# A gated cross-attention and mixture-of-experts layer on one core: the end of the kernel in the arms of its switch, router work at another point of the layers, other rows and queues for some transfers

## The chip, the cores and the metric

The kernel runs on one core of a Trainium2 chip. The metric is the device time of one execution in microseconds (us), median of several runs. A profile of one execution is used to read where the time goes; its times count from the first instruction of the span.

The core has five engines that run side by side and wait for one another through semaphores: TensorE (PE; its weight loads are shown as PEld), VectorE (DVE), ScalarE (ACT), GpSimd (POOL) and SyncE (SP). SP does no arithmetic; it issues most of the transfers. Each engine takes its instructions in order: one that waits holds all that stand behind it on its engine.

## The reference, cut to what matters

```python
# x: (16, 256, 512), ctx: (16, 256, 512); E = 8 experts, K = 2
q = layernorm(x) @ Wq;  k, v = split(ctx @ Wkv)
x = x + tanh(g_xattn) * softmax(q k^T / sqrt(512)) v
n = layernorm(x)
probs = softmax(n @ gate_w + gate_b, axis=1)        # over the tokens of a batch entry
vals, idx = top_k(probs, 2)
h = relu(n @ w1[e] + b1[e]);  h = relu(h @ w2[e] + b2[e]);  y = relu(h @ w3[e] + b3[e])
v[e] = sum over all tokens that chose e of their weight * y[e]   # one vector per expert
out = for each token the sum of v over its two experts
x = x + tanh(g_ffn) * out
```

There are 4096 tokens, so 8192 (token, expert) pairs. The kernel works out an expert only for the tokens that chose it. The sum over the tokens gives one vector of 512 numbers for each expert, and the output adds two of these vectors to every token's row. In the reference the sums are taken over the whole input (`'ebso,bse->eo'`), so nothing can be written out before the last expert is done.

## The kernel before, in words

**Attention, groups of 512 tokens.** `NG` = 8 groups (two batch entries each) are worked one after another. For a group `now` the kernel computes scores for both entries (`scores(now, 0)`, `scores(now, 1)`, L748), stores the exponentials to memory and loads them back in another layout (`send_exps`, `bring_exps`; L796, L802), forms the values (`all_values`), mixes (`mix`, matmuls L824, addition to the row L829), normalises the new rows and stores them as `tokens` (`normalise`, L205, L210), and reads them back in quarters (`xq`, L215). The group before it, `last`, goes through the router in between: `turn_rows` (a transposing DVE instruction, L226), `logits` (L236), `soften`, `divide`, `show_probs`, `choose` (13 small DVE instructions, L272 to L294), `count`, `place` (L311 to L318 and eight indirect stores on POOL, L321, which enter the tokens into `lists`).

**Experts, blocks of 528 entries.** The lists are cut into blocks of `SB` = 528 entries of one expert each. `tabulate` (L349 to L396, small DVE instructions) works out which expert and which place of the lists each block has. It is done three times, as lists fill: `tabulate_early` after group 6's attention for blocks 0 to 2 (from the copy `lists_a`), `tabulate_more` for blocks 3 and 4 (from `lists_m`), `tabulate_rest` for the rest. There are at least `NF` = 16 blocks; any beyond that (up to 7) are in a switch at the end (`tc.Switch`, L1175) whose arm 0, for none, is empty of work. In this input the arm taken is arm 0.

A block's way in: `load_tokens` (SP reads an entry of `table` into a register and loads `who`, L446), `gather` (POOL, five indirect loads L468 into `xr`), `send_rows` (store to `block`, L478 and L482), `bring_rows` (four loads `xr_q`, L487), `turn` (DVE, L226).

**A layer.** Every block runs three layers of the function `layer`. Each multiplies 512 x 512 weights with 512 x 528 rows by seven products of quarters (each eight matmuls of 128 x 264, L1019), with sums and differences on DVE ahead (`sub` for the four t, `sums` for the weights of the next layer) and additions and copies behind. The order within a layer is written out by hand (`manual_schedule` for PE, ACT, DVE and SP). The part that matters here, as PE, DVE and ACT see it:

```python
ps_y = pair("w")
for o in range(2):
    add(ps_y[o], ps_z[o], u2[:, o, :])          # DVE, L527
product(ps_x, s3, t3, False)                    # PE
for o in range(2):
    nc.scalar.copy(u3[:, o, :], ps_x[o])        # ACT, L1050
    add(out(1, 1, o), ps_z[o], u3[:, o, :])     # DVE, L527
    put(1, 1, o, out(1, 1, o))                  # ACT, L1030
product(ps_y, s4, half(1, 1), False)            # PE
# two put(0, 1, o): ACT; then `late`; then product(ps_x, part(w,1,1), t4) and two put(1, 0, o): ACT reads ps_x
```

The two banks of `ps_x` are used again by the first product of the next layer. The layer takes lists of foreign work for DVE: `first` and `second` (between the subs), `early` (after the subs), `late` (after the additions).

**Before block 0**: after the loop over groups, the last group's attention and the router of group 6 are interleaved by hand; `mix` calls `turn(held[0], rows[0], 0)` after its second tile; four matmuls at L1127 read `held[0]` ahead of block 0's first product.

**The end.** After the switch: a product and a reduction (L1218, L1223) sum the blocks of each expert, L1231 adds two parts, four transposes (L1237) and a scaling (L1241) give `v_sb`; for each of 8 groups four matmuls (L1250) form the additions, DVE adds three of the four tiles to the rows (L1259), ACT copies the fourth (L1256) and POOL adds it (L1257); one 1 MB store for each group (L1261), SP and ACT taking turns.

**The beginning.** SP issues the loads of `wq` and `wk` in turns (L588, L589); ACT's queue begins with the small loads of the gates and the router's weights (L141 to L154) and the Tanh (L144).

## Time and profile before

| | |
|---|---|
| median of three runs | 1005.53 us (1005.03 to 1010.96) |
| the profiled execution's own time | 1010.59 us |
| its span, first to last instruction | 1008.9 us |
| PE busy | 965.2 us |
| DVE busy | 695.3 us |
| ACT busy | 370.2 us |
| POOL busy | 182.6 us |
| data moved | 176.45 MB |
| mean granted TensorE clock | 0.986 |

The profiled execution is one of the longer ones: its time is near the highest of the three runs. A share of busy time is an average over stages: attention up to about 360 us, the 16 blocks from there to 972 us, the end from there. In a row of the timeline the first number is the start, the second the duration; what stands in brackets is the idle time of that engine just before, and what ended it. In the list of waits the numbers are the total in us, how often, and the longest.

### The profile page before, as it was taken

The numbers are of one execution on the slowest core, as the hardware profiler recorded it, in microseconds if no ns is written. First come the engines' busy times: TensorE is split into PE (matmuls) and PEld (weight loads), VectorE is DVE, ScalarE is ACT, GpSimd is POOL, SyncE is SP. The second block draws the span as 40 slices with busy tenths as digits, with TensorE's granted clock in tenths as the row PEclk, the third lists the DMA queues.
The fourth block names the chain that finished last, engine by engine and source line by source line (L and its number), as shares of the span: only waits on it lengthen the run. The fifth ranks groups of instructions, "written<-read, shape, count | busy, mean of one in ns | idle before, by whom it ended". The sixth has DMA issues, their size and how long they took to land. (4 is left out here: it accounts for less than half of the span.)

```text
span 1008.9 us, 12597 instructions
## 1 busy us (share of the span) xinstructions
PE 965.2 (96%) x4208; PEld 769.3 (76%) x4208; DVE 695.3 (69%) x1487; ACT 370.2 (37%) x874; POOL 182.6 (18%) x212
## 2 busy tenths in 40 slices
PE   7999999999999889999999999999999999999964
PEld 3677878778787367788788888888888888888851
DVE  3467677686777587776886676766776676676735
ACT  1222223122232124344444444444444444444421
POOL 2000330312303441205022102202202201100003
PEclk9999999999999999999999999999999999999987
DMA  7256536465475798759668667667757757756109
GB/s 265 71 166 179 135 117 186 137 179 143 137 189 129 209 237 233 202 164 177 170 201 207 164 198 199 172 195 194 182 185 194 186 181 194 199 168 150 64 5 333
DMA packets 156159, 176.45 MB, mean 175 GB/s; under 512 B 38929, under 2 KB 94225, under 8 KB 156050
## 3 DMA queue, kind: packets, MB, share of 16 engines
q1 hardware_dynamic: 145442, 153.42, 55.4%
q0 software_dynamic: 7680, 17.90, 6.9%
q10 hardware_dynamic: 2960, 4.21, 1.2%
q8 instruction: 36, 0.59, 0.2%
q14 instruction: 41, 0.34, 0.1%
HBM read 136.33 MB, written 39.77 MB: 175 GB/s over the span
## 5 line engine op out<-in xcount | busy, mean ns | idle before, releaser
L1019 PE MATMUL ps_x<-t,s 128*128 128x264 f32 x768 | 186.7, 386 | 1.6 <-ACT ps_w L1037 1.6
L1019 PEld LDWEIGHTS ps_x<-t,s 128*128 128x128 f32 x768 | 145.8, 190 | 26.9 <-ACT ps_w L1037 2.0
L468 POOL DMA_INDIRECT xr<-tokens,at_b x80 | 83.5, 1044 | 196.6 <-DMA block<-xr 174.1
L1030 ACT ACTIVATE h<-ps_w,bias 128x264 f32<-128x264 f32 x192 | 86.2, 474 | 44.2 <-PE ps_w L1019 44.2
L1019 PE MATMUL ps_z<-t,w_e 128*128 128x264 f32 x384 | 93.4, 386 | 0.5 <-DVE t L530 0.5
L527 DVE TENSOR_TENSOR ps_w<-ps_z,u 128x264 f32<-128x264 f32 x96 | 41.8, 440 | 75.5 <-ACT h L1030 75.4
L1019 PE MATMUL ps_x<-t,w_e 128*128 128x264 f32 x384 | 93.3, 386 | 0.0
L321 POOL DMA_INDIRECT lists<-pairs,idx x64 | 62.9, 983 | 162.6 <-DVE hot L314 122.4
L1041 ACT COPY u<-ps_x 128x264 f32<-128x264 f32 x96 | 36.4, 379 | 132.2 <-PE ps_x L1019 132.2
L1019 PEld LDWEIGHTS ps_z<-t,w_e 128*128 128x128 f32 x384 | 72.8, 190 | 13.4 <-DVE t L530 0.9
L1019 PEld LDWEIGHTS ps_x<-t,w_e 128*128 128x128 f32 x384 | 73.0, 190 | 12.5
L527 DVE TENSOR_TENSOR h<-ps_z,u 128x264 f32<-128x264 f32 x96 | 41.5, 432 | 56.1 <-ACT u L1050 56.1
L530 DVE TENSOR_TENSOR s<-w_e 128x512 f32<-128x512 f32 x96 | 66.1, 689 | 11.5 <-DMA w_e<-in_L_ffn_w 9.9
L1030 ACT ACTIVATE h<-h,bias 128x264 f32<-128x264 f32 x96 | 49.4, 515 | 52.6 <-DVE h L527 52.6
L1019 PE MATMUL ps_w<-h,s 128*128 128x264 f32 x256 | 62.4, 387 | 3.3 <-DVE ps_w L527 3.3
L1019 PE MATMUL ps_x<-h,w_e 128*128 128x264 f32 x256 | 62.3, 386 | 0.0
L1019 PE MATMUL ps_w<-h,w_e 128*128 128x264 f32 x256 | 62.2, 386 | 0.0
L530 DVE TENSOR_TENSOR t<-h 128x528 f32<-128x528 f32 x64 | 45.2, 706 | 20.5 <-ACT h L1030 19.8
L1019 PEld LDWEIGHTS ps_w<-h,s 128*128 128x128 f32 x256 | 48.5, 190 | 12.3 <-DVE ps_w L527 4.1
L1037 ACT COPY ps_w<-ps_x 128x264 f32<-128x264 f32 x96 | 34.8, 363 | 61.7 <-PE ps_x L1019 60.7
L748 PE MATMUL sc<-wide,wide 128*128 128x256 f32 x256 | 56.6, 379 | 0.0
L824 PE MATMUL mm<-v,eT 128*128 128x512 f32 x128 | 56.2, 592 | 0.0
(178 smaller groups left out, 1554.4 us busy)
## 6 DMA issues: line engine op xcount, KB each, us to landing
w_e<-in_L_ffn_w SPq DMA_DIRECT2D x48, 1024.0 KB, 7.3
xr_q<-block SPq DMA_DIRECT2D x64, 272.0 KB, 9.0
block<-xr SPq DMA_DIRECT2D x16, 1024.0 KB, 8.6
early<-in_x_t SPq DMA_DIRECT2D x8, 1024.0 KB, 8.1
wide<-in_ctx_t SPq DMA_DIRECT2D x8, 1024.0 KB, 6.2
x<-in_x SPq DMA_DIRECT2D x8, 1024.0 KB, 5.9
tokens<-xn SPq DMA_DIRECT2D x32, 256.0 KB, 3.6
xq<-tokens SPq DMA_DIRECT2D x32, 256.0 KB, 5.1
```

Source lines behind the costliest of these rows:

```text
L321: ins = nc.gpsimd.indirect_dma_start(out=lists, out_offset=at, in_=pairs[:, s.g * TG + t, i, :], in_offset=None)
L468: tc.keep_in_program_order(nc.gpsimd.indirect_dma_start(out=r.rows[:n, t, :], out_offset=None, in_=src, in_offset=bass.IndirectOffsetOnAxi ...
L527: nc.vector.tensor_tensor(out, a, b, ALU.add)
L530: nc.vector.tensor_tensor(out, a, b, ALU.subtract)
L748: nc.tensor.matmul(sc[:, t, :], qT[:, c, q0 : q0 + P], s.ctxT[:, c, b * S : (b + 1) * S], start=(c == 0), stop=(c == NC - 1),)
L824: nc.tensor.matmul(ps, s.eT[b][:, k, own * P : (own + 1) * P], s.v[:, b * ST + k, :], start=(k == 0), stop=(k == ST - 1),)
L1019: nc.tensor.matmul(ps[o], a[:, k, o * P : (o + 1) * P], b[:, k, :], start=(first and k == 0), stop=(k == 1), skip_group_check=True,)
L1030: nc.scalar.activation(out(a, j, o), ps, AF.Relu, bias=x.bias[:, c : c + 1])
L1037: nc.scalar.copy(ps_w[o], ps_x[o])
L1041: nc.scalar.copy(u2[:, o, :], ps_x[o])
```

## The change

In words:

- **The end in the arms.** What stood after the switch (`summed`, the transposes, the scaling, the writing out) is now a function `write_out(n)`, called in each of the eight arms. A hint of the switch's target is issued on all five engines ahead of block 15 (`tc.switch_hint`). The sum over blocks 0 to 14 (`sum_most`) stands between layers 1 and 2 of block 15. In arm 0 the last block's share is one product of 128 x 32 without a reduction. The scaling is cut in two halves, DVE and ACT.
- **The order of the last transfers.** Group 0 is stored tile by tile, group 1 in halves, the others whole, by ACT and SP in turns, the even groups' store being issued by ACT after its copy for the next group; the tile that POOL adds comes first in groups 1 to 7.
- **4 KB rows.** A partition now holds two neighbouring rows of `x`, so that loads of `x` and stores of the output move 4 KB at a time (the 256 KB stores of group 0 keep 2 KB). The host permutes `x_t` to match.
- **Queues at the beginning.** `wk` is loaded by ACT's queue, the gates' and the router's small loads come after it.
- **A new place for router work in a layer**: `mid`, after the two additions into `ps_y` and before those into `out(1, 1, o)`. The second use of `tabulate` is cut in two, block 0 and block 1, layer 1 (before: ahead of block 0); `turn_rows` of the last group goes from `early` to `mid` in block 0, layer 2; `soften` from `early` to `second` in block 1, layer 0, `divide` from `late` to `mid` there; `choose` from block 1, layer 1, `early`, to layer 2, `mid`; `place` in block 2, layer 1, from `early` to `mid`; the two parts of `tabulate_rest` in block 3, layers 0 and 1, from `late` to `mid`. The `who` and the gather for block 3 are issued after layer 1 of block 1.
- **The way into block 0.** `lists_a` is copied inside `normalise`, between the stores of `tokens` and the loads of `xq`; `turn_rows(last)` stands between the two scores of the last group; the exponentials' store and load stand ahead of the first weights; `who` and the first gather ahead of them.

The core of the diff:

```diff
     def load_x(g):
-        nc.sync.dma_start(xg[g], x_f[...].rearrange("(t p) d -> p t d", p=P))
+        nc.sync.dma_start(xg[g].rearrange("p (b k) d -> p b k d", k=ST), as_held(x_f, g))
...
-                nc.sync.dma_start(wk_sb[:, c, :], weight(wk_t)[:, c, :])
+                nc.scalar.dma_start(wk_sb[:, c, :], weight(wk_t)[:, c, :])
...
         projections()
+        load_gates()
...
-            normalise(now)
+            normalise(now, [copy_lists] if g == GA else [])
...
+        scores(now, 0)
+        turn_rows(last)
         for b in range(NA):
             who[b] = load_tokens(b)
         rows[0] = gather(0, who[0])
+        send_exps(now, 0)
+        bring_exps(now, 0)
+        scores(now, 1)
+        send_exps(now, 1)
+        bring_exps(now, 1)
         weights[0] = open_expert(0)
         load_layer(weights[0])
-        for b in range(BG):
-            scores(now, b)
-            send_exps(now, b)
-        bring_exps(now, 0)
         send_rows(rows[0])
-        bring_exps(now, 1)
         rows[1] = gather(1, who[1])
-        turn_rows(last)
         logits(last)
...
-        tabulate_more()
...
             for o in range(2):
                 add(ps_y[o], ps_z[o], u2[:, o, :])
+            for work in mid:
+                work()
             product(ps_x, s3, t3, False)
...
+        tables = tabulate_more()
         block = one(0, NF, {
...
-            "early2": [lambda: turn_rows(now)],
+            "mid1": [lambda: next(tables)], "mid2": [lambda: turn_rows(now)],
         })
...
         block = one(1, NF, {
-            "early0": [lambda: soften(now)], "late0": [lambda: divide(now)],
-            "early1": [lambda: choose(now)],
+            "second0": [lambda: soften(now)], "mid0": [lambda: divide(now)],
+            "mid1": [lambda: run(tables)], "mid2": [lambda: choose(now)],
         })
         next(block)
         show_probs(now)
+        next(block)
+        who[NA] = load_tokens(NA)
+        rows[NA] = gather(NA, who[NA])
         run(block)
-        block = one(2, NF, {"early1": [lambda: place(now)]})
+        block = one(2, NF, {"mid1": [lambda: place(now)]})
...
-        block = one(3, NF, {"late0": [lambda: next(tables)], "late1": [lambda: run(tables)]})
+        block = one(3, NF, {"mid0": [lambda: next(tables)], "mid1": [lambda: run(tables)]})
...
-            for b in range(NM, NF):
+            for b in range(NM, NF - 1):
                 run(one(b, NF))
+            tc.switch_hint({e: extras for e in (PE, DVE, ACT, POOL, SP)}, NB - NF + 1, label="rest")
+            block = one(NF - 1, NF)
+            next(block)
+            next(block)
+            vT, most = sum_most()
+            run(block)
             flush(NC)
-        for n in tc.Switch(extras, NB - NF + 1):
+        for n in tc.Switch(extras, NB - NF + 1, hint="rest"):
...
+            was = list(used)
+            write_out(n)
+            used[:] = was
```

The new functions of the end, cut:

```python
def write_out(n):
    if n:
        rest = summed(vpart[:, :, NF - 1 : NF + n], own[:, NF - 1 : NF + n, :])
    else:
        rest = top(1, NC, E)
        nc.vector.tensor_tensor(rest, <column NF-1 of vpart>, <row NF-1 of own>, ALU.mult)
    nc.vector.tensor_tensor(vT[:, :, :, :E], most, rest, ALU.add)     # broadcast
    ...                                                              # 4 transposes into halves
    nc.vector.tensor_scalar(v_sb[:, :n], halves[0][:, :n], gate[:, 1:2], None, ALU.mult)
    nc.scalar.activation(v_sb[:, n:], halves[1][:, :n], AF.Identity, scale=gate[:, 1:2])

    def store(g, t):
        b, k = divmod(t, ST)
        rows, out = xg[g].rearrange("p (b k) d -> p b k d", k=ST), as_held(o_f, g)
        if g == 0:
            nc.sync.dma_start(out[:, b, k], rows[:, b, k])
        elif g == 1:
            if k == ST - 1:
                nc.sync.dma_start(out[:, b], rows[:, b])
        elif t == TG - 1:
            (nc.sync if g % 2 else nc.scalar).dma_start(out, rows)
```

## The prediction

> **What bounds the kernel now.** I read the page's busy times first, then the list of waits for TensorE's own idle time, then the timeline around each of these waits, then the chain and the stretches of the end.
>
> ```profile
> PE 965.2 (96%) x4208; PEld 769.3 (76%) x4208; DVE 695.3 (69%) x1487; ACT 370.2 (37%) x874; POOL 182.6 (18%) x212
> ```
>
> PE is the bound: an edit gains only where PE stands idle, and costs wherever it makes PE wait. The waits of PE (engine, waited for: us in total, times, longest):
>
> ```profile
> PE mm L607 <- DMA wide<-in_wk_t: 7.1, 1, 7.1
> ...
> PE vps L1237 <- DVE room L1231: 7.0, 1, 7.0
> ...
> PE ps_w L1127 <- DVE x L829: 4.9, 1, 4.9
> ...
> PE pt L236 <- DVE xnT L226: 3.3, 1, 3.3
> ...
> PE ps_w L1019 <- DVE ps_w L527: 3.3, 2, 2.1
> ...
> PE ps_x L1019 <- ACT ps_w L1037: 1.6, 1, 1.6
> ...
> PE out_ps L1250 <- DVE room L1241: 0.9, 1, 0.9
> ...
> PE ps_z L1019 <- DVE t L530: 0.5, 1, 0.5
> ```
>
> They sum to 28.6 us, and the end without PE (993.9 to 1008.9) is the rest. Only 5.4 us (3.3 + 1.6 + 0.5) lie inside the expert blocks. The 7.0 at L1237 is explained by the chain:
>
> ```profile
> 972.30 0.07 DVEq L1308
> 972.37 3.82 issue
> 976.19 0.63 DVE room L1218
> ```
>
> DVE is done at 972.0, branches, and stands for 3.82 us with nothing to wait for. After that the store bounds (us, busy times with counts, PEclk, DMA share, GB/s):
>
> ```profile
> 984.00:986.00 2.00, 2.00 (x14) 1.16 (x12) 2.00 (x4) 0.26 (x1) 1.27 (x1) 0.75 0.55 207
> 986.00:988.00 2.00, 2.00 (x15) 0.92 (x9) 2.00 (x5) 1.17 (x2) 1.22 (x1) 1.00 1.03 373
> ...
> 1000.00:1002.00 2.00, 0.00 (x0) 0.00 (x0) 0.00 (x0) 0.00 (x0) 0.00 (x0) 0.50 1.04 368
> ```
>
> From 985 to 1007.3 the transfers are full at some 376 GB/s, so the end is: when the first byte leaves, plus 8.39 MB at that rate.
>
> **The beginning: -1.0 us.** PE starts at 7.05, when the first quarter of wk is there; its load is issued at 1.26, behind that of wq at 0.81. On ACT's queue, with the small gate loads behind it, it is issued at about 0.81: -0.45. DVE's own three operations on wq run from 4.64 to 6.04, so PE could start there, some 1.0 sooner, if wk's quarter lands with wq's. Bounds: 0 (same engines, nothing lands sooner) and -1.6 (wq sooner too). I take -1.0. The Tanh, now later, is hidden: its reader, L777, is first needed at 47.8. A rule speaks against more than the first figure: the Trainium skill, page "DMA: Bandwidth & Descriptors", section "Issuing engines are not separate DMA queues", says that transfers issued from several engines share the same 16 DMA engines and that only issue time is saved. By it the term would be -0.45 and the total below -5.9 instead of -6.4.
>
> **The way into block 0: -3.8 us.** Here lie the waits of 3.3 and 4.9.
> - The router's matmuls wait until 331.67 for `turn_rows`, which runs 329.30 to 331.61 behind the second maximum. Moved ahead of it, it can start when `xq` is there: four loads issued 320.29 to 322.20, 5.1 to landing, so 327.3; plus 2.31 is 329.6, against 328.4 when the scores end. 2.1 of 3.3 goes.
> - Ahead of the additions of L829 DVE runs `tabulate_more` from 349.10 to 354.34. Without it, additions follow PE's tiles. What is late next is `xr_q`: `turn(held[0])` needs it before the last two additions. `lists_a` is copied before the `xq` loads and not behind them, so `who` can be issued at 325.9, when the table is written (before: 328.91), and the gather some 3 us sooner. But SP now passes two round trips of exponentials (2.3 + 2.1 each) and 1 MB of weights before the store of `block`: I get that store at about 339.5 (before 342.30), its landing behind the weights, `xr_q` issued at 346.6 (before 347.31) and landed 8 later at 354.5. Turn 1.31, two additions 1.37: L1127 starts at about 357.0 instead of 360.25. That is -3.3, the 2.1 within it.
> - After the 4.9 us wait PE runs slow: the four matmuls at L1127 take 647 ns each (2.1 us), the first eight of L1019 2.76 against 1.94. After the 3.3 us wait it did not: L236's sixteen took 1.92 as always. With a wait near 3.5 left, I take a quarter of the 1.9 us: -0.5.
>
> Bounds: 0 (rows no sooner) and -7.5 (both waits nearly gone, clock kept).
>
> **The new place `mid`: +6.2 us net, the term that decides.** What follows it in a layer (timeline of block 15, layer 1):
>
> ```profile
> 953.50 0.44 DVE L527 TENSOR_TENSOR ps_w<-ps_z,u 128x264 f32<-128x264 f32 x1 [0.45 <-ACT h L1030]
> ...
> 954.29 0.43 DVE L527 TENSOR_TENSOR h<-ps_z,u 128x264 f32<-128x264 f32 x1 [0.35 <-ACT u L1050]
> ...
> 954.75 0.51 ACT L1030 ACTIVATE h<-h,bias 128x264 f32<-128x264 f32 x1 [0.50 <-DVE h L527]
> 955.17 0.36 ACT L1050 COPY u<-ps_x 128x264 f32<-128x264 f32 x1
> 955.57 0.43 DVE L527 TENSOR_TENSOR h<-ps_z,u 128x264 f32<-128x264 f32 x1 [0.85 <-ACT u L1050]
> ...
> 957.43 0.48 ACT L1030 ACTIVATE h<-ps_x,bias 128x264 f32<-128x264 f32 x1
> ...
> 958.12 1.94 PE L1019 MATMUL ps_x<-h,w_e 128*128 128x264 f32 x8
> ```
>
> At `mid` DVE idles 0.35. Work there delays the first addition into h, and ACT works in order: behind that addition stand its Relu, the second copy, the second addition, three more Relus, and last the Relu that frees `ps_x` (957.43, ends 957.91). PE's next layer starts into `ps_x` at 958.12. Where the addition is late already (480.36 in block 2) that Relu follows it by 2.89 us, against 3.15 here: 0.26 of slack. With 0.14 between the Relu's end and PE (0.2 less a hand-over) and the 0.45 by which a DVE that doesn't wait is sooner (0.34 from addition to addition, against 0.79), 0.85 us at `mid` is free, and the rest moves PE one for one.
>
> Durations, start to start, from this trace: first part of `tabulate_more` 2.86 (349.10 to 351.96), second 2.38, `choose` 2.80 (424.03 to 426.83), `place` 2.60 (from 461.56), the parts of `tabulate_rest` 2.62 (495.40 to 498.02) and 3.13 (507.36 to 510.49). Sum 16.4, less 6 x 0.85: +11.3. Free: `divide` (0.5), and `turn_rows` in block 0, layer 2 (2.3), since PE has the router's 1.92 us next, which don't use `ps_x`.
>
> Against it go the waits that the old places made: 2.08 (block 0, `turn_rows` in `early`), 1.63 (block 1, `soften`), 0.49 (block 3), and most of 1.23 in block 2, where weights landed 3.8 late and will not if PE comes later: -5.1 with 0.9 of the last. At their old places `choose`, `place` and the second part of `tabulate_rest` cost PE nothing. Bounds of the term: -5.4 (`mid` costs nothing) and +8.
>
> In block 1 SP reads the table for block 3 only when `mid` of layer 1 has written it, at about 430 on the old clock; behind it stand the weights of layer 2, which went out at 432.2 before: hidden, with 2 us to spare.
>
> **The end: -7.8 us.**
> - The stall of 3.82 goes: after the first branch the engines were in arm 0 within 0.5 us; the one that stalls is the second, out of the arm, and the work now comes before it. At its new place it lies behind the last store's issue, under some 8 us of transfers. -3.8. If that cover fails it is back.
> - The last block's sum 0.62 + 0.42 becomes one of some 0.19 (128 x 32, as L294): -0.85; the scaling 0.75 becomes two halves of 0.45 side by side: -0.3. `sum_most` (1.03 + 0.65 before) goes where DVE idles 1.32 before the t of layer 2, 2 us ahead of need: nothing.
> - Group 0's first store leaves after one DVE addition (982.53) and not after POOL's (983.98): -1.4. Adding 256 KB takes 0.6, moving it 0.7, so the transfers stay full.
> - PE's clock was 0.50 there after 7 us of idling; with 2.5 us it may stay: 0 to -0.8, I take -0.4.
> - 4 KB rows for 7.34 of 8.39 MB. No row shows such a store. The nearest, 4.2 KB pieces of `wbc`, are slower (0.54 MB in 26.2% of 6.5 us: 319 GB/s); copies of 18.8 KB reached 442 in their best slice (`lists_a`). Bounds +3.5 and -2.9; near the first lies a single transfer's start and end, so I take -1.0.
>
> Sum -7.75. Bounds -2.5 and -11.
>
> **Sum.** -1.0 - 3.8 + 6.2 - 7.8 = -6.4 us. From the profiled execution's 1010.59 (span 1008.9 and 1.69 around it) that gives 1004.2; this execution is 5 above the median of the runs, whose 1005.53 gives 999.1.
>
> **Rivals.**
> 1. *`mid` is free.* The values added there, out(1, 1), are needed only by the second product of the next layer, and DVE is idle 31% of the time. Against: the Relus in one line on ACT. The term is -5.1 instead of +6.2: 987.8.
> 2. *The rows of block 3 come too late (slower).* Their gather was issued at 413 to 419, 26 us ahead of their store at 445.2; now `who` is read at 430.4, the gather ends at 439.6 and lands 8.4 later, at 448, when the store is due, with PE 3.5 later. If POOL holds it as long as its longest wait for `block` (17.3 us), it lands near 465; SP waits with weights and `xr_q` behind it, which have 6 us to spare: some 11 us, and 1010. The total is slower than before from 455 on.
> 3. *The branch still costs.* The exit, or a fetch in block 15 displaced by the hint, takes 3.8 again: 1002.9.
>
> **Numbers.** The forecast 0.50 (its own range 993 to 1003), rival 1 0.25, rival 2 0.12, rival 3 0.13. Low end 987 from rival 1, high end 1007 between rivals 3 and 2. One per cent, about what a measurement tells, is 10 us: faster by more holds for nearly all of rival 1 and the forecast's low end, 0.33; slower by more for a part of rival 2, 0.07; within it 0.60.
>
> **What would show it.** PE waits of 1.5 to 2.3 us for an ACT Relu at the start of the layer after each of the six `mid` works (`ps_x` L1019 <- ACT h), 11 us in all; no 3.82 issue in the chain; first store some 10 us after the last product (before 13.2); the end at more than 376 GB/s; L1127's wait near 3.5. No such PE waits, or a wait of SP for the gather into `xr` in block 2, would make the forecast wrong.

## The result, and the profile after

The changed kernel takes 1014.89 us (median of 6 runs, 1012.79 to 1018.80) against 1007.65 of the kernel before (median of 6, 1005.03 to 1010.96). The ratio is 1.0076, with a 95% interval of 1.0047 to 1.0105: slower, where the forecast was 6.4 us faster. The profiled execution took 1013.73 us (span 1011.9). The six runs of the changed kernel spread with PE's mean granted clock (three at 0.987 to 0.988 took 1012.8 to 1013.7, three at 0.983 to 0.984 took 1016.1 to 1018.8), while the 87 runs of the kernel before that stand beside the experiments show no such relation.

The busy time of PE, from the first part of the page of the changed kernel:

```profile
PE 965.3 (95%) x4208; PEld 767.1 (76%) x4208; DVE 693.9 (69%) x1485; ACT 369.2 (36%) x875; POOL 185.5 (18%) x212
```

PE is busy for as long as before (965.2). So the loss is to be looked for in its idle time, and the list of waits of PE in the changed kernel (engine, waited for: us in total, times, longest) says where:

```profile
PE ps_w L1235 <- DVE x L834: 14.5, 1, 14.5
PE mm L612 <- DVE early L608: 6.1, 1, 6.1
PE ps_x L1028 <- ACT h L1039: 5.8, 6, 1.0
PE ps_x L1028 <- ACT u L1061: 2.7, 5, 1.1
PE ps_x L1188 <- DVE room L1180: 2.3, 1, 2.3
PE pt L242 <- DVE xnT L232: 0.7, 1, 0.7
PE out_ps L1216 <- ACT room L1193: 0.6, 1, 0.6
```

Line numbers have moved: L612 was L607, L242 was L236, L1235 was L1127, L1028 was L1019, L1188 was L1237. Three of the four parts went the way that was forecast: PE starts 0.95 sooner, the wait for the sum at the end is 2.3 and not 7.0, and the new stalls of `mid` are there, 8.5 us in this list. The fourth, the way into block 0, went the other way: the router's wait is 0.7 and not 3.3, but the wait ahead of block 0, forecast at 3.5, is 14.5. The queue of SP shows why. The rows of block 0 go through it twice: they are stored to `block`, and when that store has landed they are loaded again as `xr_q`. Its timeline in the changed kernel (start, time to issue):

```profile
339.74 0.40 SPq L523 DMA_DIRECT2D w_e<-in_L_ffn_w  x1
340.32 0.38 SPq L483 DMA_DIRECT2D block<-xr  x1
340.75 0.49 SPq L487 DMA_DIRECT2D block<-xr  x1
354.04 1.93 SPq L492 DMA_DIRECT2D xr_q<-block  x4
356.21 1.36 SPq L523 DMA_DIRECT2D w_e<-in_L_ffn_w  x2
```

the same store and load in the kernel before:

```profile
342.30 0.38 SPq L478 DMA_DIRECT2D block<-xr  x1
342.77 0.45 SPq L482 DMA_DIRECT2D block<-xr  x1
...
347.31 1.91 SPq L487 DMA_DIRECT2D xr_q<-block  x4
```

and two pieces of the chain that ended last in the changed kernel (start, us, what):

```profile
340.75 13.21 DMA block<-xr
355.48 7.82 DMA xr_q<-block
```

The store of `block` is issued two microseconds earlier than before (340.75 and not 342.77) and lands 6.7 later: 13.2 us, where the old order needed 4.5. `xr_q` can only be issued then, and DVE, which has nothing else to do, waits 13.6 us for it.

The end, in stretches (us; busy time with counts of PE, PEld, DVE, ACT, POOL; PEclk, DMA share, GB/s):

```profile
984.00:986.00 2.00, 1.38 (x12) 0.74 (x15) 0.48 (x1) 0.47 (x1) 0.00 (x0) 1.00 0.04 8
...
988.00:990.00 2.00, 2.00 (x14) 0.90 (x10) 2.00 (x5) 0.59 (x1) 2.00 (x3) 1.00 1.03 381
...
1000.00:1002.00 2.00, 0.00 (x0) 0.00 (x0) 0.69 (x2) 0.12 (x1) 1.26 (x1) 0.64 1.05 397
```

PE's clock stays at 1.00 behind the wait (before, in the stretch where the transfers began, 0.75), and the full stretches move 381 to 414 GB/s, where those of before moved 368 to 397. From the last product to the end of the span it is 30.3 us, 38.1 before.

### The profile page after: what moved, and what is told of

Read it like the earlier page. It is cut to its first block, busy times and chain, and to the rows that moved or that the text cites. A ratio compares the mean times of both kernels' runs of the same rounds, so it can differ in the third digit from the quotient of the medians.

```text
span 1011.9 us, 12632 instructions
## 1 busy us (share of the span) xinstructions
PE 965.3 (95%) x4208; PEld 767.1 (76%) x4208; DVE 693.9 (69%) x1485; ACT 369.2 (36%) x875; POOL 185.5 (18%) x212
## 4 chain that ended last, share of the span: by engine, by line
PE 85%; DVE 5%; DMA 3%; ACT 2%; POOL 2%; issue 1%; SPq 1%; DVEq 0%; ACTq 0%; POOLq 0%
PE ps_x L1028 32%; PE ps_w L1028 16%; PE mm L665 14%; PE ps_z L1028 8%; PE sc L753 5%; PE mm L829 4%; ACT h L1039 2%; PE mm L612 2%; PE mm L740 1%; DMA block<-xr 1%; PE pt L242 1%; PE out_ps L1216 1%; POOL lists L327 1%; DMA xr_q<-block 1%; DMA exps<-ex 1%
## 5 line engine op out<-in xcount | busy, mean ns | idle before, releaser
L1028 PE MATMUL ps_x<-t,s 128*128 128x264 f32 x768 | 186.6, 386 | 0.0
L1028 PEld LDWEIGHTS ps_x<-t,s 128*128 128x128 f32 x768 | 145.9, 190 | 25.0
L473 POOL DMA_INDIRECT xr<-tokens,at_b x80 | 86.3, 1079 | 195.7 <-DMA block<-xr 173.1
L1028 PE MATMUL ps_x<-t,w_e 128*128 128x264 f32 x384 | 94.9, 388 | 2.7 <-ACT u L1061 2.7
L1028 PE MATMUL ps_z<-t,w_e 128*128 128x264 f32 x384 | 93.3, 386 | 0.0
L1028 PEld LDWEIGHTS ps_x<-t,w_e 128*128 128x128 f32 x384 | 72.4, 190 | 17.4 <-ACT u L1061 5.4
L1028 PEld LDWEIGHTS ps_z<-t,w_e 128*128 128x128 f32 x384 | 73.0, 190 | 12.5
L1028 PE MATMUL ps_x<-h,w_e 128*128 128x264 f32 x256 | 62.8, 388 | 4.8 <-ACT h L1039 4.8
L1028 PE MATMUL ps_w<-h,w_e 128*128 128x264 f32 x256 | 62.2, 386 | 0.0
L1028 PE MATMUL ps_w<-h,s 128*128 128x264 f32 x256 | 62.2, 386 | 0.0
L1028 PEld LDWEIGHTS ps_x<-h,w_e 128*128 128x128 f32 x256 | 46.6, 189 | 16.4 <-ACT h L1039 6.9
```

The source lines that it names most:

```text
L473: tc.keep_in_program_order(nc.gpsimd.indirect_dma_start(out=r.rows[:n, t, :], out_offset=None, in_=src, in_offset=bass.IndirectOffsetOnAxi ...
L1028: nc.tensor.matmul(ps[o], a[:, k, o * P : (o + 1) * P], b[:, k, :], start=(first and k == 0), stop=(k == 1), skip_group_check=True,)
```

## Experiments

All ratios are to the kernel before, run on the same chip; "changed kernel" is the one above. Waits are those of each run's own trace, in us, by the line numbers of the changed kernel.

| run | ratio (95%) | wait L242 | wait L1235 | waits for ACT in L1028 |
|---|---|---|---|---|
| changed, again | 1.0069 (1.0049 to 1.0088) | 1.0 | 13.8 | 8.5 |
| block first | 1.0021 (1.0006 to 1.0037) | 1.0 | 9.7 | 8.5 |
| scatter later | 1.0051 (1.0027 to 1.0074) | 1.1 | 10.2 | 8.6 |
| rows first | 1.0003 (0.9986 to 1.0020) | 1.3 | 3.2 (+1.9 for weights) | 8.6 |
| rows first, scatter later | 1.0009 (0.9994 to 1.0024) | 0.9 | 2.9 (+0.9) | 8.8 |
| whole old order | 0.9958 (0.9945 to 0.9971) | 3.3 | 1.0 | 8.6 |
| old queue, early `turn_rows` | 0.9979 (0.9963 to 0.9995) | 1.0 | 3.4 | 8.5 |
| old places | 1.0002 (0.9984 to 1.0020) | 1.2 | 14.1 | 1.4 |
| `mid` behind | 0.9969 (0.9955 to 0.9983) | 0.8 | 14.1 | 0 |
| 2 KB rows | 1.0091 (1.0057 to 1.0125) | 1.4 | 14.0 | 8.6 |
| no hint | 1.0081 (1.0056 to 1.0105) | 1.0 | 14.4 | 8.5 |
| rows first + places | 0.9902 (0.9868 to 0.9937) | 1.1 | 3.5 (+1.1) | 0 |
| ... + weights ahead | 0.9881 (0.9855 to 0.9907) | 1.0 | 3.9 | 0 |
| old queue + places | 0.9887 (0.9871 to 0.9904) | 0.9 | 3.4 | 0.2 |
| whole old order + places | 0.9873 (0.9854 to 0.9893) | 3.3 | 1.0 | 0.3 |

### The kernel before, a second profile

> The kernel before, once more, for a second profile of it. The profiled execution of before took 1010.59 us where its other runs had a median of 1005.5, so the traces of before and after differ by 3 us where the runs differ by 7. If that execution was a slow one, this profile's time is 1005 to 1007, and its waits of PE show which of those read before were larger than usual (3.3 at L236, 4.9 at L1127, 2.1 and 1.6 at L1019). If profiled executions are slower in general, it is again about 1010. Ratio 1.000.

The profiled execution took 1011.01, ratio 0.9995 (0.9982 to 1.0008). Neither guess holds cleanly: the profiled execution is the highest of its ten, but profiled executions of other kernels (1007.14 of 1005.81 to 1012.36, 996.73 of 996.73 to 999.24) are not high. The runs of before in all these comparisons lie between 1004.3 and 1011.7; what makes the whole of that spread stays open. What the second profile does show is which waits were those of one execution. Its waits of PE:

```profile
PE pt L236 <- DVE xnT L226: 3.9, 2, 3.3
PE ps_w L1127 <- DVE x L829: 3.8, 1, 3.8
PE ps_w L1019 <- DVE ps_w L527: 1.5, 2, 0.8
PE ps_x L1019 <- ACT ps_w L1037: 1.4, 1, 1.4
```

The 2.1 us that the forecast put down to `turn_rows` in `early` of block 0 is gone, though `turn_rows` stands at the same place. In the first profile DVE's waits between 385 and 402 show what was different, a late transfer that `turn_rows` reads; the second has no such wait:

```profile
DVE xnT L226 <- DMA xq<-tokens: 2.5, 1, 2.5
```

### The way into block 0

Block first. The edit:

```
-        weights[0] = open_expert(0)
-        load_layer(weights[0])
         send_rows(rows[0])
+        weights[0] = open_expert(0)
+        load_layer(weights[0])
```

> The changed kernel with one thing different: `block`'s store (send_rows) stands ahead of the first MB of weights on SP's queue, and not behind it. Theory 1 (the new hand order puts the store behind the weights; in the changed kernel it was issued at 340.75 and landed at 353.98, PE then waited 14.5 us at L1235): the store lands within 5 us of its issue, at about 345, `xr_q` at about 353, the wait at L1235 falls from 14.5 to 2 to 5 us, and the ratio to the kernel before from 1.0076 to about 0.997. Theory 2 (the scatter of `place`, which now runs at the same time as the store, slows it): the store still lands at 350 or later, the wait stays above 9 us, and the ratio above 1.003.

Scatter later. The edit moves `place(last)` from behind `count(last)` to behind `figures_left = mix(...)`:

> The changed kernel with one thing different: `place` of group 6 comes only after the additions in front of L1235, so that its scatter no longer runs beside `block`'s store; the weights stay ahead of the store. It puts 2.6 us of DVE in front of block 0's first sums. Theory 1 (behind the weights): the store still lands at about 352, the wait at L1235 stays at 12 to 15 us, some 2 us are lost behind it, and the ratio is 1.007 to 1.011. Theory 2 (the scatter): the store lands at about 346, the wait falls under 7 us, and the ratio is about 1.001.

Neither theory got its numbers. The chain of the first of these two kernels, then of the second:

```profile
339.50 7.03 DMA block<-xr
...
348.06 10.98 DMA xr_q<-block
```
```profile
341.30 8.08 DMA block<-xr
...
350.91 8.69 DMA xr_q<-block
```

The 13.2 us of the store (11.5 in the second profile of the changed kernel) fall to 7.0 in the one and to 8.1 in the other. So taking away the weights ahead of it or the scatter beside it wins some 5 to 6 us, and what is left still keeps it at 7 to 8, where a store with neither takes 4.5. (In the first of the two the weights go out 2 us behind the store, so the 7.0 need not be the scatter's alone.) With the store first, the time comes back on the second leg: `xr_q` then shares the DMA engines with the weights, the scatter and the next gather (11.0 from its last issue to DVE). This widened theory 1: what counts is all that shares the engines with the rows, on both legs.

Rows first:

```
         send_exps(now, 1)
+        send_rows(rows[0])
         bring_exps(now, 1)
+        bring_rows(rows[0])
         weights[0] = open_expert(0)
         load_layer(weights[0])
-        send_rows(rows[0])
...
-        bring_rows(rows[0])
```

> The changed kernel with one thing different: on SP's queue the store of `block` stands ahead of the second fetch of exponentials, and the fetch of `xr_q` ahead of all the weights of block 0, so that nothing large is ahead of the rows on their whole way. After the two runs before (block's store put ahead of the first MB of weights: landed 7.5 us after its issue, `xr_q` 12.5 after its own, wait 9.75; scatter moved away alone: 8.5 and 10.2, wait 10.2) theory 1 is widened: the rows lose time to whatever shares the DMA engines with them, on both legs. It expects the store at about 337 to land by 342, `xr_q` by 351, the wait at L1235 at 2 to 4 us, and a ratio of about 0.997. The rival, that the scatter of `place` is what slows `xr_q`, and the weights only the store, expects `xr_q` to take 11 us or more still, a wait of 5 us or more, and 0.999 or higher. A second rival: the weights of block 0, now last, come too late in their turn and PE waits 3 us or more behind L1235.

The store is issued at 337.85 and `xr_q` at 342.21 (4.4 us), DVE turns the rows at 352.47, and the wait is 3.2, as the widened theory said; the ratio is higher than it said, 1.0003, since the weights, now last, cost 1.9 of their own. 7 us are won. The same with the scatter out of the way:

> The rows-first kernel (`mid` as changed) with `place` of group 6 behind the additions in front of L1235. In the rows-first run `xr_q` still took 10.2 us from its issue to DVE's transposition (342.2 to 352.4). If the scatter that runs beside it is the reason, it takes 8.5 us or less now and the wait at L1235 falls from 3.2 to under 2 us; if the weights and the second gather behind it are, it stays at 9.5 us or more. Either way some 2 us of `place` stand ahead of block 0's first sums and come back there.

`xr_q` goes out at 342.79 and is turned at 352.14: 9.4 us from first issue to DVE (10.3 before), the wait 2.9. By its own measure (8.5, or 9.5 and more) this falls between the two answers; the scatter has a part of 1 us on that leg at most, and the ratio doesn't change.

The old order of the way, without `tabulate_more`, and with one thing of the change left in it: `lists_a` is still copied inside `normalise`, so that `who` is loaded at 325.15 and not at 328.91:

> The changed kernel with the whole old order of the way into block 0 (weights, then both stores of exponentials, then `block`, `turn_rows` late), but without `tabulate_more` there, which stays in `mid`. Theory 1: `block` goes alone again (before: issued 342.8, landed 347.3) and the last packet of `xr_q` comes at 355 to 356; the wait at L1235 falls from 14.5 to between 3 and 4.5 us and the 3.3 us in front of the router's matmuls come back: 7 to 8 us won, ratio 1.000 to 1.001. It also says how much `tabulate_more` cost at its old place: the wait was 4.9 and 3.8 us in the two profiles of before; the forecast had 1.2 us for it, and if `xr_q` itself is as late as the wait, it is nothing. Rival: without `tabulate_more` the additions follow PE at once, the wait falls under 2.5 us, and the ratio is below 0.999.

The rival is right: the wait at L1235 (L1234 in this kernel) falls to 1.0, and the kernel is 11 us faster than the changed one (ratios 0.9958 against 1.0069), 4 us faster than before. Its SP timeline:

```profile
328.46 0.37 SPq L523 DMA_DIRECT2D w_e<-in_L_ffn_w  x1
328.93 0.97 SPq L801 DMA_DIRECT2D exps<-ex  x2
...
338.68 0.38 SPq L483 DMA_DIRECT2D block<-xr  x1
339.15 0.45 SPq L487 DMA_DIRECT2D block<-xr  x1
...
343.61 1.91 SPq L492 DMA_DIRECT2D xr_q<-block  x4
```

The first MB goes out at 328.5, ten microseconds ahead of `block`, when the gather is not yet back, and has landed by 334.5; the store takes 4.4 us; and this with a store that leaves only 1.6 us sooner than in the changed kernel. Against the kernel before, the wait is 2.9 to 3.9 us shorter (4.9 and 3.8 in its two profiles, 1.0 here). The forecast had 1.2 for this, beside the router's 2.1. Two things are behind it, and no run takes them apart: DVE has no `tabulate_more` ahead of its additions (it follows PE's tiles from 350.5, where before it started on them at 354.3, straight behind `tabulate_more`), and the earlier `who` brings the rows sooner (`xr_q` goes out at 343.6 and not at 347.3).

Only the queue's order old, `turn_rows` early as in the change:

```
+        weights[0] = open_expert(0)
+        load_layer(weights[0])
+        scores(now, 0)
+        turn_rows(last)
         send_exps(now, 0)
-        bring_exps(now, 0)
         scores(now, 1)
         send_exps(now, 1)
+        bring_exps(now, 0)
+        send_rows(rows[0])
         bring_exps(now, 1)
-        weights[0] = open_expert(0)
-        load_layer(weights[0])
-        send_rows(rows[0])
```

> The changed kernel with the old order of SP's queue on the way into block 0 (first weights, both stores of exponentials, first fetch, `block`, second fetch), but with `turn_rows` early as in the change. Theory 1, that the whole loss of the way is the queue's order and that the early `turn_rows` is a gain of its own: L1235 waits about 1 us as in the run with the whole old order, L242 about 1 and not 3.3, and the ratio is about 0.993 to 0.994. Rival: the early `turn_rows` holds up DVE's maximum for the second scores, the second store of exponentials leaves 2 us later with `block` behind it, the wait at L1235 is 3 us or more, and the ratio is 0.996 or higher.

The two waits in this kernel:

```profile
PE ps_w L1235 <- DVE x L834: 3.4, 1, 3.4
...
PE pt L242 <- DVE xnT L232: 1.0, 1, 1.0
```

With the late `turn_rows` they were 1.0 and 3.3 (the run before this one): 4.4 and 4.3 us in sum. The early `turn_rows` doesn't hold up the exponentials, as the rival said (`block` leaves 0.6 us later), and it wins nothing either: PE comes 2.3 us sooner to a place where `xr_q` says when it goes on (DVE waits for it until 352.76, the chain there reads 345.56, 7.08, DMA xr_q<-block). Theory 1 was right on the queue and wrong on a gain of its own.

### The places of the router's works

Old places: `tabulate_more` ahead of block 0, `soften`, `choose`, `place` and `turn_rows` in `early`, `divide` and the rest of the tables in `late`, the rows of block 3 fetched where they were before.

> The changed kernel with the router's works back at the old places: both parts of `tabulate_more` ahead of block 0, `soften`, `choose`, `place` and `turn_rows` in `early`, `divide` and the tables' rest in `late`, the rows of block 3 fetched where they were; the order of the way into block 0 stays the new one. Theory 1: the eleven waits of 0.4 to 1.1 us at L1028 (8.4 us in all) go and the old ones (2.1, 1.6, 0.5, 1.2 us) come back, so 3 us are won; `tabulate_more` hides in the 14.5 us in which DVE waits for `xr_q` anyway, and that wait stays; ratio about 1.005. A rival, that the new places are the whole loss: the ratio falls to 0.998 or lower. The forecast's own size of this term, 6.2 us, would give 1.0015.

6.7 to 7.4 us are won (1.0002 against 1.0069 and 1.0076, each good to some 2 us), near the forecast's 6.2 and twice what theory 1 expected. Of the old waits only 1.4 and 0.5 came back, as in the second profile of before.

`mid` behind the additions, one line of `layer`:

```
-            for work in mid:
-                work()
             product(ps_x, s3, t3, False)
             for o in range(2):
                 nc.scalar.copy(u3[:, o, :], ps_x[o])
                 add(out(1, 1, o), ps_z[o], u3[:, o, :])
                 put(1, 1, o, out(1, 1, o))
+            for work in mid:
+                work()
```

> The changed kernel with one line of its layer moved: the works of `mid` come behind DVE's two additions into out(1, 1) and not ahead of them (0.9 us of DVE later); all works, blocks and layers are the same, and so is the order of the way into block 0. The theory of the forecast (the additions hold up ACT's second copy and the Relus behind it, and these hold ps_x): all waits of PE for ACT's copy and Relu in blocks 0 to 3 (eleven, 8.3 us) go, up to 0.5 us appear for a DVE t or s behind the longest work, and the ratio falls from 1.0076 to about 1.000. Rival: DVE has no 2.4 to 3.1 us free anywhere in a layer, and the same 5 us or more appear as waits for DVE's t, s or sums; ratio 1.005 or more.

Its waits of PE inside the blocks:

```profile
PE ps_z L1028 <- DVE t L535: 1.1, 2, 0.6
```

No wait for ACT is left; by this list the same work, 0.9 us later in DVE's order, costs 1.1 us and not 8.5. The ratio, 0.9969, is below what was expected: 10 us less than the changed kernel, of which the lists explain 7.4. The rest is what such a list leaves out. It counts a wait from the end of the last matmul, and in a running stream the next one starts before that end. The chain of the changed kernel shows the distance from product to product, in block 3, layer 1, and in a later layer without a wait (start, us):

```profile
505.25 2.05 PE ps_x L1028 x8
507.30 1.78 PE ps_z L1028 x8
...
520.29 2.05 PE ps_x L1028 x8
522.34 1.78 PE ps_z L1028 x8
...
534.79 1.78 PE ps_z L1028 x8
...
547.25 1.78 PE ps_z L1028 x8
```

From one `ps_z` to the next it is 15.04 us with the two waits and 12.46 without. That is 2.58 for waits that the list has as 1.08 and 0.97, so each costs some 0.27 more than listed. Measured like this, the six layers with a stalling work in `mid` take 14.38, 13.78, 14.50, 14.10, 14.22 and 15.04 us, 11.2 more than the same layers without it (12.46, the second 12.56). With `mid` behind the additions two waits are left, which cost 1.6. So 9.6 of the 10 us are explained.

How the stall comes about, from the changed kernel's timeline of block 3, layer 0 (in brackets: idle before, and what ended it):

```profile
500.39 1.52 DVE L368 TENSOR_TENSOR until<-until,blocks 128x1 f32<-128x1 f32 x8
...
501.83 0.43 DVE L532 TENSOR_TENSOR h<-ps_z,u 128x264 f32<-128x264 f32 x1
502.29 0.51 ACT L1039 ACTIVATE h<-h,bias 128x264 f32<-128x264 f32 x1 [2.67 <-DVE h L532]
502.71 0.36 ACT L1061 COPY u<-ps_x 128x264 f32<-128x264 f32 x1
...
503.12 1.16 PE L1028 MATMUL ps_x<-t,w_e 128*128 128x264 f32 x4 [0.36 <-ACT u L1061]
...
504.72 0.85 ACT L1039 ACTIVATE h<-ps_x,bias 128x264 f32<-128x264 f32 x2
...
505.25 0.94 PE L1028 MATMUL ps_x<-h,w_e 128*128 128x264 f32 x3 [0.97 <-ACT h L1039]
```

ACT stands 2.67 us for DVE's addition, and everything behind it is late. PE waits twice: for ACT's second copy, which still reads a bank of `ps_x` that the last product writes (0.36 here, 1.08 behind the longest work, none behind the shortest), and at the next layer for the last Relu. This second wait is 0.97 in all six layers, whatever the work's length. The forecast had only the second.

### The end

Rows of 2 KB:

```
-        return rows[g * G : (g + 1) * G, :].rearrange("(b p k) d -> p b k d", p=P, k=ST)
+        return rows[g * G : (g + 1) * G, :].rearrange("(b k p) d -> p b k d", p=P, k=ST)
```

(and the columns of `x_t` in the old order)

> The changed kernel with the old layout of the rows of x and of the output (row t*128+p on partition p, so that each contiguous piece is 2 KB and not 4 KB). Forecast of the term: the transfers at the end are 1.0 us longer, with bounds of 2.9 longer and 3.5 shorter; read from the first output packet to the last. A rival: the rate at the end is bounded by the DMA engines' bytes and not by the pieces, and the time from first to last packet is the same within 0.3 us.

From the first output packet to the last it is 23.67 us with 2 KB rows and 22.65 with 4 KB, in every profile of a 4 KB kernel: 1.0, as forecast. Two stretches near the end of the store with 2 KB rows:

```profile
1004.00:1006.00 2.00, 0.00 (x0) 0.00 (x0) 1.61 (x3) 0.59 (x1) 0.88 (x2) 1.00 1.03 367
1008.00:1010.00 2.00, 0.00 (x0) 0.00 (x0) 0.00 (x0) 0.00 (x0) 0.00 (x0) 0.50 1.03 375
```

But the kernel before, with 2 KB rows and whole groups, needed 22.40: with the new order of the stores the same rows take 1.3 longer, more than the longer rows give back. Most of that is lost at the end and not at the single tiles of the start: the first tenth of the bytes is through after 2.4 us before and 2.3 in both others, 99% after 22.0 before, 22.4 with the new order and 2 KB, 21.3 with 4 KB, and the last hundredth takes 0.4, 1.2 and 1.3.

No hint (`tc.switch_hint` taken out, `tc.Switch` without `hint`):

> The changed kernel without the hint of the branch's target (the sum and the output stay inside the arms). The forecast put the gain of 3.8 us on the place of the work (ahead of the branch out of the arm, which was what stalled) and nothing on the hint: the time from the last product to the last packet stays at 30.3 us within 0.5. The rival: without the hint the first branch stalls some 3.8 us ahead of the sum of the last block, the wait at L1188 grows from 2.3 to about 6, and the end from 30.3 to about 34 us, ratio 1.011.

30.35 us from the last product to the end, with the hint 30.34; ratio 1.0081. The hint makes no difference here. The 3.8 us were the branch out of the arm, and went because the work now comes ahead of it.

### Both repairs together

Rows first, and the works moved: `tabulate_more`'s parts to `late` of layer 1 of blocks 0 and 1, `choose` and `place` to `early` of layer 1, the rest of the tables to `late`.

> The order of the run before this one (rows ahead of the weights) and, with it, the router's works out of `mid`: the parts of `tabulate_more` in `late` of layer 1 of blocks 0 and 1, `choose` and `place` in `early` of layer 1, the rest of the tables in `late`; `soften`, `divide` and `turn_rows` stay at their new places. If the two losses are separate, they add up: 7 us less than the rows-first kernel alone, no wait of PE for a Relu at L1028 in blocks 0 to 3, and a ratio of about 0.990. If a `late` place merely moves the stall (the additions in `late` come just ahead of the next layer's t), PE waits 0.5 us or more for a DVE t or s in three or more of these layers, and the ratio is 0.993 or higher.

0.9902: they add up (6.6 for the order and 10 for the places in the single runs, 16.7 together). With the first weights moved to where the old order had them:

> The kernel with the rows first and the router's works out of `mid`, with the first MB of block 0's weights moved right behind the first gather, ahead of the exponentials, where the old order had it. The last run left 3.5 us at L1235 and 1.1 us for these weights. Theory 1: at 329 to 336 the DMA engines have room, the 1.1 us go, `xr_q` no longer shares with the first MB and lands 1 us sooner: 1.5 to 2.5 us won, ratio about 0.988. Rival: the MB slows the gather of block 0 and the first store of exponentials, `block` leaves 2 us later or more, and the ratio is 0.990 or higher.

0.9881. The 1.1 for the weights goes, `xr_q` comes no sooner (wait 3.9), and the two intervals overlap. With the old queue:

> The same, with the router's works out of `mid` as in the earlier run that had rows first (`tabulate_more` in `late` of layer 1, `choose` and `place` in `early`, the rest of the tables in `late`). If the parts add up, the eleven waits for ACT go (8.3 us less 0.5 for one DVE t), and the ratio is 0.985 to 0.986, the fastest of all. If the rows-first order was as good (0.990, and 0.988 with the weights ahead), it is 0.988 or higher.

0.9887, short of the 0.986: its waits are those expected (L242 0.9, L1235 3.4, one DVE t 0.5), so this order is no better than rows first with the weights ahead. With the whole old order:

> The whole old order of the way into block 0 (with turn_rows late) and the router's works out of `mid`. If what separates the late from the early `turn_rows` is PE's clock behind the wait at L1235 (1.7 us for the twelve matmuls), this kernel has waits of about 3.3 and 1.0 us, the twelve matmuls take 2.8 and not 4.5 us, and the ratio is 0.987 or lower, under the 0.9887 of the kernel with the early one. If it is chance, the ratio is 0.989 to 0.991, since the two waits together are the same 4.3 us.

0.9873, the lowest ratio: 994.21 us (994.07 to 995.26), 13 us less than the kernel before. Two of its waits of PE:

```profile
PE pt L242 <- DVE xnT L232: 3.3, 1, 3.3
...
PE ps_w L1234 <- DVE x L834: 1.0, 1, 1.0
```

The reason given for it ahead of the run does not hold, though. The twelve matmuls behind L1234 do take 2.8 and not 4.5 us, but PE's clock is lost at the other wait instead: the sixteen matmuls of L242 and the eight behind them take 7.2 us here and 5.6 behind a wait of 0.9. Wait and clock together are the same in both orders, the intervals of the two pairs (0.9958 and 0.9979, 0.9873 and 0.9887) overlap, and whether the late `turn_rows` is better by 1 to 2 us stays open.

The changed kernel beside these runs:

> The changed kernel once more, beside the others. Its first comparison gave 1.0076 (1.0047 to 1.0105). If the parts measured in the other runs are complete (the order of the way 0.0104 to 0.0118 against the old one, the places of the works 0.0074 to 0.0107), it lies at 1.005 to 1.008; below 1.004 it would say that the chips differ and that the gains of the two undone parts are smaller than their ratios.

1.0069: the first comparison holds on another chip.

## Why the prediction was wrong

**Beginning, -1.0: right.** 7.05 to 6.10; 6.84 in the second profile of before, 5.6 to 6.5 in the others of the new beginning. PE now waits for DVE (L608), as forecast.

**Way into block 0, -3.8: the step that failed, +6.9.** In PE's waits it is 0.71 + 14.54 against 3.31 + 4.89, less 0.2 of clock. Each of three sub-steps was off.
- "I get that store at about 339.5, its landing behind the weights, `xr_q` issued at 346.6": the store went out at 340.3 and 340.8, and `xr_q` at 354.0, 13.7 us after the store's first issue where the working had 7.1. The working added some 2 us for the weights to a store's own time and had nothing for the scatter of `place`. Both are in flight with the store: taking away the one or the other brought its 13.2 us to 7.0 and 8.1, and with the weights behind `xr_q` or long landed it took 4.4.
- The router's wait fell by 2.6 (2.1 forecast), but that is no gain, since PE then stands at L1235 for `xr_q` for as much longer (4.4 against 4.3 us in sum).
- Leaving out `tabulate_more` and copying `lists_a` earlier, valued at 1.2 beside the router's 2.1, were worth 2.9 to 3.9 together with the old order. They were the good part of this edit, and the new queue order hid it: with the old order the way costs 4.3 us of waits, and not the 15.3 of the changed kernel.

**`mid`, +6.2: right in sign, too small; the waits taken away were mis-sized.** From product to product the six stalls cost 11.2 us, the forecast's 11.3, so that of a work of 2.4 to 3.1 us some 0.87 is free, the forecast's 0.85. (The list of waits, with 8.5, shows less.) Part of this is luck: the forecast had only one of the two waits, the Relu's, and not the one for the second copy. The waits taken away were 2.4 by the same measure, 1.9 in the list, and not 5.1: the 2.1 of block 0 was a late transfer of one execution, and so was part of the 1.6 in block 1 (1.4 in the second profile); the 1.2 in block 2 was 0.7 there, and did not come back with the old places. 11.2 less 2.4 is 8.8; undoing it won 6.7 to 7.4 by the ratios, whose intervals reach to it. That `mid` is free (rival 1) is refuted.

**End, -7.8: right, 38.13 to 30.34, in part by luck.** The first packet leaves 6.25 us after the last product (14.15 before), 7.9 sooner where the sum had 6.75. PE's clock, which stayed up in that execution, is about 0.95 of it and not 0.4: in the profiles in which it fell the first packet left at 7.1 to 7.6, and the end took 31.2 to 31.7. The transfers took 22.65 and not a microsecond less than the 22.40 of before. The 4 KB rows gave the 1.0 that was put down for them, a figure picked between bounds of +3.5 and -2.9, and the new order of the stores took 1.3, for which the sum had nothing. So what the transfers did not give, the clock and the earlier first packet did.

**Rivals.** The rows of block 3 did not come late: between 400 and 470 SP waits nowhere for a gather. The branch does not cost again (no idle piece of 3.8 us in the chain). The case that came, the way into block 0 growing, was in none of them, and the bounds of that term (0 and -7.5) left out a loss: the edit put 1 MB and two round trips ahead of the transfer that the end of the stage hangs on, and the lower bound should have been what these cost if they didn't overlap.

**The sum and its base.** The four terms as the traces have them add up to +7.0 (-0.95 + 6.9 + 8.8 - 7.8), where the forecast had -6.4; the runs say +7.6 (4.7 to 10.6). Of the difference of 13.4, the way into block 0 is 10.7 and the waits that `mid` was to take away are 2.7. The forecast also counted from 1005.53, the median of three runs, while later medians of the same kernel were 1006.7 to 1008.7: some 2 us of the miss in the time itself are that.

## What to carry to other kernels

When a hand-written queue order is changed, follow the one transfer on which the next stage hangs through both of its legs, and price everything that is in flight beside it, other queues too, not only what stands ahead of it. A wait removed ahead of a later wait is worth nothing until the later one is shorter; add up the waits up to the next transfer before counting a gain. Foreign work in an engine's gap is free or not by what is queued behind it on the other engines: here 0.9 us later in the order was worth nearly 10 us. A list of waits says where an engine stood, and too little of what it cost: measure from the start of one piece of work to the start of the next. And a wait read in a single profile may belong to that execution alone; of the 5.1 us counted here, some 2.6 stood in a second profile of the same kernel.

## What the runs showed of the hardware

**A wait near 3.3 us may or may not cost PE its clock.** Behind the wait of 3.31 us in front of the router's sixteen matmuls these took 1.92 us in the first profile of before (as always), and 3.06 in the second:

```profile
331.67 1.92 PE L236 MATMUL pt<-xnT,gw 128*32 128x256 f32 x16 [3.31 <-DVE xnT L226]
```
```profile
332.10 3.06 PE L236 MATMUL pt<-xnT,gw 128*32 128x256 f32 x16 [3.31 <-DVE xnT L226]
```

The forecast read the first and took it for a rule. Of four profiles with this wait, three lost 1.65 us over the sixteen matmuls and the eight behind them, and one lost nothing. Waits of 0.7 to 1.4 us at L242 and L1234 cost nothing in any profile. Waits of 2.9 to 14.5 us at L1235 (L1127) cost the twelve matmuls behind them 1.5 to 3.0 us, and their length doesn't say how much: 1.5 behind 14.5 in the changed kernel, 2.7 behind 14.4 in the run without the hint, 1.7 behind 3.4. Around this wait the granted clock stands at 0.50 for 3.4, 6.8, 10.2, 13.7 or 17.1 us, and what is lost is what of such a stretch lies behind PE's restart: in the changed kernel it lasts from 355.4 to 369.1, and PE is back at 366.1. The Trainium skill, page "TensorE: Matmul & The Clock Gate", section "Part 1: The HAM clock gate", has an idle window of about 3.4 us that runs freely, so that the loss varies from run to run; the two rows above agree.

**Transfers to memory.** 8.39 MB left in 22.65 us, 370 GB/s, and the full stretches of 2 us lie between 381 and 414 with 4 KB rows and between 367 and 397 with 2 KB rows. The Trainium skill, page "DMA: Bandwidth & Descriptors", section "Where 436 GB/s comes from", puts what the memory gives one core, half of a stack's rate, at about 358 GB/s; with one core at work the measurement is higher, and decides.

**Late weights.** In nine of the eighteen profiles PE waits once or twice for 0.2 to 1.5 us in one of the later blocks, for DVE's additions, and always at the same product, the sixth of a block's last layer: in block 7 in six profiles, in block 13 in three, in blocks 5 and 12 in one each. Where the chain runs through such a place, it goes to a load of weights: in the block-first run one of 12.28 us at 661.1 with a wait of 1.5 behind it, and one of 12.35 at 849.3 with 1.0. This can be a part of the spread between executions.
